# Keeping the first experts' last chunk back and adding it inside the second attention

## The chip, the cores and the metric

The kernel runs on one core of one Trainium2 chip. The metric is the device time of one execution in microseconds (us); the time given for a kernel is the median of several runs. A profiled execution of the same program gives the trace from which the lines below are copied.

## The reference

The input x has 16 batches of 256 rows of 128 channels, all in float32. Four residual steps follow each other, and each works on a layer norm of x:

```python
x = x + attn_a(layernorm(x))
x = x + ffn(layernorm(x))
x = x + attn_b(layernorm(x))
x = x + ffn(layernorm(x))
```

`attn_a` and `attn_b` are softmax attentions with 16 heads of 8 channels; `attn_b` adds a relative position term to the scores. The feed-forward step (the "experts") is the same function both times:

```python
logits = einsum('bld,ed->ble', x, gate_weight)          # 8 experts
kth    = sort(logits.reshape(-1))[4 * 128 * 6 - 1]
gates  = logits * (logits >= kth)
h      = gelu(einsum('bld,ehd->bleh', x, w1) + b1)       # 512 hidden
y      = einsum('bleh,edh->blde', h, w2) + b2
out    = einsum('blde,ble->bld', y, gates)
```

## The kernel before

**State.** x stays in SBUF for the whole kernel as 16 tiles `x0` to `x15`, one for each batch, rows on partitions. The experts work in the transposed layout, channels on partitions, in 8 chunks of two batches (512 rows): chunk 7 holds batches 14 and 15.

**Stages.** The program runs attention a, the first experts, attention b and the second experts, each in pools of its own. `experts(last, ...)` is called with `last=False` for the first and `True` for the second. For each of 64 pairs of chunk and expert (c, e) there are four hidden units (`h_unit`, line 1078: a matmul of 512 columns and a gelu on ACT, line 1080) and one output (`y_unit`, line 1089: four matmuls accumulated in a PSUM bank `py`). `gated` (lines 1201 to 1205) then adds the bias, multiplies by a broadcast row of gates `gb`, and sums into `acc` of the chunk, on DVE. The `gb` tiles come by DMA from DRAM on SP's queue (`broadcast_gates`, line 1182, seven buffers). The first 16 pairs are computed ahead, in the tail of the attention in front, and kept as `raw` tiles.

**The end of a chunk.** `residual` (lines 1225 to 1234) transposes the sum back with four transposes on PE (line 1228) into a PSUM bank `f_pr`, and adds it to the two x tiles on DVE (line 1231). For chunks 0 to 6 this is put one step later, behind the next pair's matmuls. The last pair of chunk 7 goes through `last_in_halves` (lines 1207 to 1223): its `y_unit` is done in two halves of 256 columns, and each half has its own gating (line 1217), sum (line 1220), two transposes and one add.

**Attention b.** `attention_b` opens the pool `b_w` before the first experts begin. `begin` puts the first pieces of batches 0 to 2 between the matmuls of the last 12 pairs of the first experts. `run` opens the pools `b_4` (SBUF) and `b_ps` (PSUM) after the experts' pools are closed; the first instruction that uses a bank of `b_ps` waits for the last reader of the closed PSUM pool. The order on the five engines in `run` is the order in which the code is written. It has 128 units, 8 for each batch: in a unit U, `scores` issues 16 matmuls in the 64x64 tiling of PE (line 876) into a two-bank tile `b_s` (three buffers), a maximum on DVE (line 886), and four exponentials on ACT (line 891); `turn`, written two units later, transposes the result on DVE (line 901). The dictionary `table` puts the other steps of a batch at fixed units: `first` at unit 0 of a batch (queries and keys of the next batch, line 718, into a one-bank tile `b_m`, two buffers), `second` at unit 4, and so on. x14 and x15 are read by attention b only for the layer norms and sums of batches 14 and 15.

Of the kernel before, what the change touches and what calls it, by code (L numbers as in the profile page):

```python
# [10 lines left out]
F32 = mybir.dt.float32  # L11
I32 = mybir.dt.int32
AF = mybir.ActivationFunctionType
ALU = mybir.AluOpType
# [4 lines left out]
P = 128  # L19
NB, T, C = 16, 256, 128  # L20
# [8 lines left out]
CH = 512  # L29
NCHUNK = NB * T // CH  # L30
# [48 lines left out]
def hybrid_kernel(ctx: ExitStack, tc: tile.TileContext, io):  # L79
    nc = tc.nc  # L80
# [5 lines left out]
    def load(name, shape, queue, src=None):  # L86
        t = cpool.tile(shape, F32, tag=name, name=name)
        queue.dma_start(t, io[name] if src is None else src)
        return t
# [4 lines left out]
    xs = [load("x0", [P, T // P, C], nc.sync, xr[0])]  # L94
# [23 lines left out]
    def const(name):  # L118
        lo, hi = CONSTS[name]
        return head[:, lo:hi]  # L120
# [7 lines left out]
    ident = const("ident")  # L128
# [516 lines left out]
    def attention_b(outer):  # L645
# [10 lines left out]
        wpool = outer.enter_context(tc.tile_pool(name="b_w", bufs=1))  # L656
# [24 lines left out]
        def values_tile(pool, i):  # L681

            va = pool.tile([P, NK, NJ, DH, NG], F32, tag=f"va{i}", name=f"b_va{i}")
            nc.gpsimd.memset(va, 0.0)
            vas.append(va)

        values_tile(wpool, 0)
        mask_h, mask_q = const("mask_h"), const("mask_q")
        NH2, NN = NH // 2, NQB // 2
        rows_of, xnTs, batch, vz, tall = {}, {}, {}, {}, {}  # L690
# [156 lines left out]
        def run(place, filling):  # L847
            with ExitStack() as st:
                main(st, place, filling)

        def main(st, place, filling):
            pool = st.enter_context(tc.tile_pool(name="b_4", bufs=1))
            psum = st.enter_context(tc.tile_pool(name="b_ps", bufs=1, space=PSUM))
# [44 lines left out]
            def turn(U):  # L898

                half, i = divmod(U, NU // 2)  # L900
                nc.vector.transpose(  # L901
                    pT[:, half % 2, 4 * i : 4 * i + 4].rearrange("p n k h q -> p (n k h q)"),
                    probs.pop(U).rearrange("p u r k -> p (u r k)"),
                )
# [99 lines left out]
            total = NB * NU  # L1004
# [23 lines left out]
            def for_batch(f, b, *rest):  # L1028
                if 0 <= b < NB:
                    f(b, *rest)  # L1030
# [11 lines left out]
                6: lambda b: for_batch(ahead_rows, b + 3),  # L1042
                7: lambda b: for_batch(ahead_spread, b + 1),
            }

            own_at = {0: 2, 1: 2, 2: 1, 4: 2, 5: 2, 6: 2, 8: 2, 9: 2, 10: 1, 12: 2, 13: 2}
            done = 0
            for U in range(total + 2 * NU + 1):
                b, i = divmod(U, NU)
                table.get(i, lambda b: None)(b)  # L1050
                if U < total:
                    scores(U)
                while done < min(total, U - 1):
                    turn(done)
                    done += 1
                if U >= total:
                    place["h"] = (epool, 5, psum, "ss", 3)
                    place["y"] = (psum, "ss", 3)
                    place["raw"] = (epool, 4)
                    for _ in range(own_at.get(U - total, 0)):  # L1060
                        own.append(next(filling))

        return begin, run


    def bank(psum, tag, name, bufs):
# [7 lines left out]
    def h_unit(place, c, e, k):  # L1074
        pool, bufs, psum, tag, mb = place["h"]
        ph = bank(psum, tag, f"ph{c}_{e}_{k}", mb)
        m = e * NHC + k
        nc.tensor.matmul(ph, w1[:, m * P : (m + 1) * P], xn2[c], start=True, stop=True)  # L1078
        hT = pool.tile([P, CH], F32, tag="hT", name=f"hT{c}_{e}_{k}", bufs=bufs)
        nc.scalar.activation(  # L1080
            hT, ph, AF.Gelu_apprx_tanh, bias=b1[:, m : m + 1], scale=1.0
        )
        return hT

    def y_unit(place, c, e, hs, width=CH, part=""):
        psum, tag, mb = place["y"]
        py = bank(psum, tag, f"py{c}_{e}{part}", mb)
        for k in range(NHC):
            nc.tensor.matmul(  # L1089
                py[:, 0:width], w2[:, e * NHC + k, :], hs[k], start=k == 0, stop=k == NHC - 1  # L1090
            )
        return py
# [19 lines left out]
                    yield  # L1112
            prev = (c, e, hs)

    def experts(last, place, raw, filling, middle):
        with ExitStack() as st:
            hpool = st.enter_context(tc.tile_pool(name="f_h", bufs=1))
            pool = st.enter_context(tc.tile_pool(name="f_2", bufs=2))
            psum = st.enter_context(tc.tile_pool(name="f_ps", bufs=1, space=PSUM))
# [58 lines left out]
                kth.append(f)  # L1178

            def broadcast_gates(c, e):  # L1180
                gb = pool.tile([P, CH], F32, tag="gb", name=f"gb{c}_{e}", bufs=7)
                nc.sync.dma_start(
                    gb.rearrange("p (t k) -> p t k", k=P),
                    gd[c * 4 * NE : (c + 1) * 4 * NE, :]
                    .rearrange("(t e) k -> e t k", e=NE)[e]
                    .partition_broadcast(P),
                )
                return gb

            accs = {}  # L1190

            def gated(c, e, y, bias):

                gb = broadcast_gates(c, e)
                if e == 0:
                    accs[c] = pool.tile([P, CH], F32, tag="acc", name=f"acc{c}", bufs=2)
                    dst = accs[c]
                else:
                    dst = pool.tile([P, CH], F32, tag="gy", name=f"gy{c}_{e}")
                if bias is None:  # L1200
                    nc.vector.tensor_tensor(dst, y, gb, ALU.mult)
                else:
                    nc.vector.scalar_tensor_tensor(dst, y, bias, gb, ALU.add, ALU.mult)  # L1203
                if e:
                    nc.vector.tensor_tensor(accs[c], accs[c], dst, ALU.add)

            def last_in_halves(c, e, hs):

                gb = broadcast_gates(c, e)
                pys = [  # L1210
                    y_unit(place, c, e, [h[:, half * T : (half + 1) * T] for h in hs], T, half)
                    for half in range(2)
                ]
                for half, py in enumerate(pys):
                    cols = slice(half * T, (half + 1) * T)
                    gy = pool.tile([P, CH], F32, tag="gy", name=f"gy{c}_{e}_{half}")
                    nc.vector.scalar_tensor_tensor(  # L1217
                        gy[:, cols], py[:, 0:T], b2[:, e : e + 1], gb[:, cols], ALU.add, ALU.mult
                    )
                    nc.vector.tensor_tensor(  # L1220
                        accs[c][:, cols], accs[c][:, cols], gy[:, cols], ALU.add
                    )
                    residual(c, (half,))
# [34 lines left out]
            total = NCHUNK * NE  # L1258
            prev, due, ready = None, 0, []
            for i in range(EARLY, total + 1):  # L1260
                c, e = divmod(i, NE)
                hs, now, ready = None, ready, []
                if i < total:
                    hs = [h_unit(place, c, e, k) for k in range(NHC)]
                if middle is not None and i >= total - 12 and i % 2 == 0:
                    next(middle(psum), None)
                if due < EARLY:
                    gated(*divmod(due, NE), raw[due], None)
                    due += 1
                    if due % NE == 0:  # L1270
                        ready.append(due // NE - 1)
                if i == total:
                    last_in_halves(*prev)
                elif prev is not None:
                    gated(
                        prev[0], prev[1], y_unit(place, *prev),
                        b2[:, prev[1] : prev[1] + 1],
                    )
                    if prev[1] == NE - 1:
                        ready.append(prev[0])  # L1280
                for done in now:
                    residual(done)
                prev = (c, e, hs)
            for done in ready:
                residual(done)

    epool = ctx.enter_context(tc.tile_pool(name="epool", bufs=1))
# [1 line left out]
    def fill():  # L1289

        place, raw = {}, []
        return place, raw, early(place, raw)

    ahead = fill()
    attention_a(*ahead[::2])
    with ExitStack() as st:
        begin, run = attention_b(st)
        experts(False, *ahead, begin)
        ahead = fill()
        run(*ahead[::2])  # L1300
    experts(True, *ahead, None)


def _spread(v, extra):
# [73 lines left out]
```

## Time and profile before

| what | value |
|---|---|
| time, median of 3 runs | 1542.66 us (1542.0 to 1543.3) |
| time of the profiled execution | 1539.13 us |
| its span, first to last instruction | 1537.3 us |
| granted TensorE clock, mean | 0.999 |
| first experts: last transposes (line 1228) of chunk 7 | 741.04 and 742.53 us |
| attention b: first scores (line 876) | 744.59 us |
| attention b: last turn (line 901) starts | 1082.8 us |
| busy share of the span: PE, DVE, ACT, POOL | 99%, 52%, 55%, 26% |

PE is shown as busy nearly everywhere, because the durations of pipelined matmuls are drawn long and overlap each other. The start times of instructions say more: the distance from one start to the next is what an instruction took of PE. In rows of the trace, a float32 matmul counts twice (two passes) and a transpose once, so that a `py` of four matmuls is a row of 8, and the scores of one unit are 32. In brackets behind a row stands how long the engine had been idle before it, and what ended the wait.

### The profile page before, as it was taken

To read this page: it belongs to the slowest core of one execution; us is meant where nothing else is said; L and a number is where in the kernel's file an instruction comes from. 1 tells how busy PE (TensorE), PEld (TensorE's weight loads), DVE (VectorE), ACT (ScalarE), POOL (GpSimd) and SP (SyncE) were. 2 spreads that over 40 slices of the span, in tenths; PEclk is the share of its full clock that TensorE was granted. 3 is DMA by queue.
4 is the path that set the end of the run, shared out by engine and by line. 5 is a ranking of instruction groups with operands and counts; after the bars stand their busy time and mean duration, and the time that the engine had idled before them with its cause. 6 is when DMAs were issued, how large, how long until landed. Compare 5 with 4: busy or idle time off the path is not lost. (4 is left out here: it accounts for less than half of the span.)

```text
span 1537.3 us, 30882 instructions
## 1 busy us (share of the span) xinstructions
PE 1524.0 (99%) x12292; PEld 858.5 (56%) x12292; DVE 800.1 (52%) x1624; ACT 838.7 (55%) x2092; POOL 405.9 (26%) x521
## 2 busy tenths in 40 slices
PE   9999999999999999999999999999999999999998
PEld 6777777544444444444677777777444444444444
DVE  6887877345133312121699999999353143212222
ACT  4666666644443334343688888888544433434342
POOL 6332331200001000003388988886100000000000
PEclk9999999999999999999999999999999999999999
DMA  3511110000322111111122222221002133211110
GB/s 97 156 33 29 36 36 16 2 7 4 76 71 80 50 39 38 38 41 28 24 56 58 50 51 48 55 57 37 8 1 62 44 84 82 51 45 39 44 41 7
DMA packets 174127, 69.91 MB, mean 45 GB/s; under 512 B 74520, under 2 KB 173600, under 8 KB 173728
## 3 DMA queue, kind: packets, MB, share of 16 engines
q1 hardware_dynamic: 173408, 67.54, 18.8%
q8 instruction: 97, 1.59, 0.4%
q10 hardware_dynamic: 576, 0.41, 0.1%
q14 instruction: 46, 0.38, 0.1%
HBM read 50.88 MB, written 12.58 MB: 41 GB/s over the span
## 5 line engine op out<-in xcount | busy, mean ns | idle before, releaser
L1080 ACT ACTIVATE hT<-ph,head 128x512 f32<-128x512 f32 x512 | 351.0, 687 | 419.4 <-PE ph L1078 416.9
L1078 PE MATMUL ph<-xn,w 128*128 128x512 f32 x1024 | 464.3, 594 | 1.1 <-ACT hT L1080 1.1
L1089 PE MATMUL py<-hT,w 128*128 128x512 f32 (+1 forms) x1040 | 461.1, 586 | 1.0 <-ACT logits L977 0.5
L1089 PEld LDWEIGHTS py<-hT,w 128*128 128x128 f32 x1040 | 196.6, 190 | 237.3 <-issue 230.6
L1078 PEld LDWEIGHTS ph<-xn,w 128*128 128x128 f32 x1024 | 191.4, 190 | 228.5 <-issue 224.7
L1203 DVE SCALAR_TENSOR_TENSOR gy<-py,head,gb 128x512 f32<-128x512 f32 x82 | 61.6, 751 | 425.5 <-PE py L1089 425.5
L891 ACT ACTIVATE b_pr<-b_s,b_nm 128x256 f32<-128x256 f32 x512 | 235.5, 473 | 58.7 <-DVE b_nm L886 58.4
L447 DVE TENSOR_REDUCE a_nm<-a_s 128x2 f32<-128x512 f32 x256 | 158.6, 683 | 51.8 <-PE a_t L470 50.1
L886 DVE TENSOR_REDUCE b_nm<-b_s 128x4 f32<-128x1024 f32 x128 | 152.7, 1193 | 20.9 <-PE b_s L876 20.6
L876 PE MATMUL b_s<-b_kT,b_qd 64*64 64x256 f32 x1024 | 159.8, 382 | 0.0
L901 DVE STREAM_TRANSPOSE b_pT<-b_pr 128x1024 f32<-128x1024 f32 x128 | 157.1, 1228 | 0.0
L876 PE MATMUL b_s<-strip,b_qb 64*64 64x256 f32 x2048 | 156.6, 376 | 0.0
L876 PE MATMUL b_s<-b_kS,b_qd 64*64 64x256 f32 x1024 | 156.5, 382 | 0.0
L476 ACT ACTIVATE a_pT<-a_t 128x512 f32<-128x512 f32 x256 | 132.5, 603 | 31.8 <-PE a_t L470 31.7
L470 PE MATMUL a_t<-a_qa,a_qk 32*128 32x256 f32 x1024 | 134.5, 394 | 0.7 <-DVE a_nm L447 0.6
L766 POOL TENSOR_TENSOR b_qd<-b_qsel,head 128x512 f32<-128x512 f32 x64 | 84.1, 1337 | 178.5 <-DMA b_qsel<-b_qT 169.7
L442 PE MATMUL a_s<-a_qk 32*128 32x256 f32 x1024 | 130.3, 390 | 0.4 <-DVE a_nm L447 0.4
L153 POOL TENSOR_SCALAR ve<-mv 128x2 f32<-128x2 f32 x64 | 14.8, 231 | 425.1 <-DVE mv L150 415.1
L442 PEld LDWEIGHTS a_s<-a_qk 32*128 32x128 f32 x1024 | 92.1, 185 | 23.5 <-issue 15.3
L891 ACT ACTIVATION_READ_ACCUMULATOR b_pr<-b_s,b_nm 128x1 f32 x512 | 104.3, 204 | 0.0
L470 PEld LDWEIGHTS a_t<-a_qa,a_qk 32*128 32x128 f32 x1024 | 100.1, 185 | 4.8 <-issue 1.7
L162 POOL TENSOR_SCALAR xn<-x,mv,rstd 128x128 f32<-128x128 f32 x126 | 99.7, 800 | 6.6
(175 smaller groups left out, 1430.9 us busy)
## 6 DMA issues: line engine op xcount, KB each, us to landing
gb<-gd SPq DMA_DIRECT2D x128, 256.0 KB
w<-in_w SPq DMA_DIRECT2D x2, 2048.0 KB
a_qks<-a_qkc SPq DMA_DIRECT2D x15, 256.0 KB
a_qk<-a_qks SPq DMA_DIRECT2D x60, 64.0 KB
x<-in_x SPq DMA_DIRECT2D x16, 128.0 KB
b_qs<-b_qT SPq DMA_DIRECT2D x64, 32.0 KB
b_qsel<-b_qT SPq DMA_DIRECT2D x64, 32.0 KB
b_z<-b_qs SPq DMA_DIRECT2D x16, 128.0 KB
```

The lines of the kernel that those rows point to most:

```text
L162: (last or nc.gpsimd).tensor_scalar(xn[:, t, :], xs[b][:, t, :], mv[:, t, 0:1], rstd[:, t : t + 1], ALU.subtract, ALU.mult,)
L442: nc.tensor.matmul(sc[:, t, :], q[b][rows, g, t * P : (t + 1) * P], k[b][rows, g, :], start=True, stop=True,)
L447: nc.vector.tensor_reduce(nms[G % 4][:, :, j, 0:1].rearrange("p t o -> p (t o)"), sc, AX.X, ALU.max, negate=True,)
L470: nc.tensor.matmul(sc[:, t, :], k[b][rows, g, t * P : (t + 1) * P], qaug[G][rows, :], start=True, stop=True,)
L476: nc.scalar.activation(pT, sc, AF.Exp)
L876: nc.tensor.matmul(sc[64 * c : 64 * c + 64, r, u, :], (qb_[rows, at, c] if rel else qd[rows, at, x]).rearrange("p h q -> p (h q)"), strip[ ...
L886: nc.vector.tensor_reduce(nm, sc, AX.X, ALU.max, negate=True)
L891: nc.scalar.activation(pr[:, u, r, :], sc[:, r, u, :], AF.Exp, bias=nm[:, r, u : u + 1], scale=1.0, accum_out=sums[b][:, n : n + 1],)
L901: nc.vector.transpose(pT[:, half % 2, 4 * i : 4 * i + 4].rearrange("p n k h q -> p (n k h q)"), probs.pop(U).rearrange("p u r k -> p (u r ...
L1078: nc.tensor.matmul(ph, w1[:, m * P : (m + 1) * P], xn2[c], start=True, stop=True)
L1080: nc.scalar.activation(hT, ph, AF.Gelu_apprx_tanh, bias=b1[:, m : m + 1], scale=1.0)
L1089: nc.tensor.matmul(py[:, 0:width], w2[:, e * NHC + k, :], hs[k], start=k == 0, stop=k == NHC - 1)
```

## The change

The tile `late` (512 float32 on each partition) is added to `b_w`, the pool of attention b that is open during the first experts. In the first experts, the sum of chunk 7 is built in `late` in place of a tile `acc7`. The last pair goes through `gated` with a whole `y_unit`, no longer in halves, and the first experts end there: the residual of chunk 7 is not made by them. In `run`, at U = 2 (the third unit), ahead of that unit's scores, `add_late` transposes `late` with four transposes into a `b_m` tile and adds the two halves to x14 and x15. To make room, the first experts have six `gb` buffers in place of seven. The second experts are as they were.

```diff
@@ -685,6 +685,8 @@
             vas.append(va)
 
         values_tile(wpool, 0)
+
+        late = wpool.tile([P, CH], F32, tag="late", name="b_late_sum")
         mask_h, mask_q = const("mask_h"), const("mask_q")
         NH2, NN = NH // 2, NQB // 2
         rows_of, xnTs, batch, vz, tall = {}, {}, {}, {}, {}
@@ -1042,12 +1044,28 @@
                 6: lambda b: for_batch(ahead_rows, b + 3),
                 7: lambda b: for_batch(ahead_spread, b + 1),
             }
+            def add_late():
+
+                pr = psum.tile([P, 2 * T], F32, tag="m", name="b_late", bufs=2)
+                for t in range(4):
+                    nc.tensor.transpose(
+                        pr[:, t * P : (t + 1) * P], late[:, t * P : (t + 1) * P], ident
+                    )
+                for j in range(2):
+                    b = NB - 2 + j
+                    nc.vector.tensor_tensor(
+                        xs[b], xs[b],
+                        pr[:, j * T : (j + 1) * T].rearrange("p (t c) -> p t c", c=C), ALU.add,
+                    )
+
 
             own_at = {0: 2, 1: 2, 2: 1, 4: 2, 5: 2, 6: 2, 8: 2, 9: 2, 10: 1, 12: 2, 13: 2}
             done = 0
             for U in range(total + 2 * NU + 1):
                 b, i = divmod(U, NU)
                 table.get(i, lambda b: None)(b)
+                if U == 2:
+                    add_late()
                 if U < total:
                     scores(U)
                 while done < min(total, U - 1):
@@ -1060,7 +1078,7 @@
                     for _ in range(own_at.get(U - total, 0)):
                         own.append(next(filling))
 
-        return begin, run
+        return begin, run, late
 
 
     def bank(psum, tag, name, bufs):
@@ -1112,7 +1130,8 @@
                     yield
             prev = (c, e, hs)
 
-    def experts(last, place, raw, filling, middle):
+    def experts(last, place, raw, filling, middle, late):
+
         with ExitStack() as st:
             hpool = st.enter_context(tc.tile_pool(name="f_h", bufs=1))
             pool = st.enter_context(tc.tile_pool(name="f_2", bufs=2))
@@ -1178,7 +1197,7 @@
                 kth.append(f)
 
             def broadcast_gates(c, e):
-                gb = pool.tile([P, CH], F32, tag="gb", name=f"gb{c}_{e}", bufs=7)
+                gb = pool.tile([P, CH], F32, tag="gb", name=f"gb{c}_{e}", bufs=7 if last else 6)
                 nc.sync.dma_start(
                     gb.rearrange("p (t k) -> p t k", k=P),
                     gd[c * 4 * NE : (c + 1) * 4 * NE, :]
@@ -1193,7 +1212,10 @@
 
                 gb = broadcast_gates(c, e)
                 if e == 0:
-                    accs[c] = pool.tile([P, CH], F32, tag="acc", name=f"acc{c}", bufs=2)
+                    if c == NCHUNK - 1 and not last:
+                        accs[c] = late
+                    else:
+                        accs[c] = pool.tile([P, CH], F32, tag="acc", name=f"acc{c}", bufs=2)
                     dst = accs[c]
                 else:
                     dst = pool.tile([P, CH], F32, tag="gy", name=f"gy{c}_{e}")
@@ -1269,7 +1291,7 @@
                     due += 1
                     if due % NE == 0:
                         ready.append(due // NE - 1)
-                if i == total:
+                if i == total and last:
                     last_in_halves(*prev)
                 elif prev is not None:
                     gated(
@@ -1281,7 +1303,7 @@
                 for done in now:
                     residual(done)
                 prev = (c, e, hs)
-            for done in ready:
+            for done in ready if last else ():
                 residual(done)
 
     epool = ctx.enter_context(tc.tile_pool(name="epool", bufs=1))
@@ -1294,11 +1316,11 @@
     ahead = fill()
     attention_a(*ahead[::2])
     with ExitStack() as st:
-        begin, run = attention_b(st)
-        experts(False, *ahead, begin)
+        begin, run, late = attention_b(st)
+        experts(False, *ahead, begin, late)
         ahead = fill()
         run(*ahead[::2])
-    experts(True, *ahead, None)
+    experts(True, *ahead, None, None)
 
 
 def _spread(v, extra):
```

In the built programs the order of the instructions changes in these places and no other. On PE, the eight matmuls of the two half `y_unit`s become four of 512 columns, the four transposes leave the end of the first experts, and four stand between the scores of units 1 and 2. On DVE, the last pair has one gating and one sum, and the two adds to x14 and x15 stand between the maxima of units 1 and 2. On SP's queue, the last three `gb` transfers of the first experts stand later: `gb7_5` and `gb7_6` behind the transfers `b_qs0`, `b_qsel0`, `b_z0` and `b_kS0` of attention b's batch 0, and `gb7_7` behind `b_vs0` and `b_vz0`. ACT and POOL keep their order. The two banks of `b_m` change places from the second `b_m` tile on.

## The prediction

> **What bounds the kernel now.** I read the page first, then the order of time at the seam between the first experts and attention b on PE and DVE, then the waits inside attention b.
>
> From the page, busy time by engine and the chain that ended last:
>
> ```profile
> PE 1524.0 (99%) x12292; PEld 858.5 (56%) x12292; DVE 800.1 (52%) x1624; ACT 838.7 (55%) x2092; POOL 405.9 (26%) x521
> ...
> PE 27%; DVE 1%; issue 0%; DVEq 0%
> ```
>
> The chain covers only the second experts (27% and 1% of the span), so it says nothing of the seam, and PE's 99% is drawn from overlapping durations. The seam has to be read row by row. PE in order of time:
>
> ```profile
> 735.44 5.76 PE L1089 MATMUL py<-hT,w 128*128 128x512 f32 x21
> 741.04 0.38 PE L1228 MATMUL f_pr<-head,acc 128*128 128x128 f32 x2
> 742.53 0.41 PE L1228 MATMUL f_pr<-head,acc 128*128 128x128 f32 x2 [1.11 <-DVE acc L1220]
> 743.52 1.13 PE L718 MATMUL b_m<-b_xnT,b_w 128*128 128x256 f32 x4 [0.58 <-DVE x L1231]
> 744.59 0.43 PE L876 MATMUL b_s<-b_kT,b_qd 64*64 64x256 f32 x1
> ```
>
> PE ends the last outputs at 741.20, then stands idle twice, 1.11 and 0.58 us, for the sums and adds of DVE. The first matmul of attention b (line 718) starts at 743.52, 2.32 us after the outputs. DVE at the same place, and its first maximum:
>
> ```profile
> 737.79 0.75 DVE L1203 SCALAR_TENSOR_TENSOR gy<-py,head,gb 128x512 f32<-128x512 f32 x1 [5.39 <-PE py L1089]
> ...
> 741.24 0.48 DVE L1217 SCALAR_TENSOR_TENSOR gy<-py,head,gb 128x256 f32<-128x256 f32 x1 [0.78 <-PE py L1089]
> ...
> 743.05 0.42 DVE L1231 TENSOR_TENSOR x<-x,f_pr 128x256 f32<-128x256 f32 x1 [0.66 <-PE f_pr L1228]
> 746.67 1.22 DVE L886 TENSOR_REDUCE b_nm<-b_s 128x4 f32<-128x1024 f32 x1 [3.20 <-PE b_s L876]
> ```
>
> Line 718 starts 0.05 us after the last add ends (743.05 + 0.42 = 743.47): the add to x15 is the last reader of the closed PSUM pool. Inside attention b the waits from 765 to 1090 us show who paces it:
>
> ```profile
> ACT b_pr L891 <- DVE b_nm L886: 55.9, 117, 1.4
> DVE b_nm L886 <- PE b_s L876: 16.5, 27, 0.9
> ```
>
> ACT waits 117 times for DVE's maximum; DVE itself waits only 16.5 us of 325. In the windows view DVE is busy 93.83 of the 100 us from 900 to 1000. Attention b is paced by DVE, and the seam by the turns between PE and DVE.
>
> **The change, part by part.**
>
> *The seam.* What is removed is the way from the last output through sum, transposes and add, at the end of the first experts. A whole `py` takes as long as two halves: eight passes started at 734.15 and the next eight at 737.58, 3.43 us later, and the two halves ended at 741.20. The whole `py7_7` therefore starts at 737.58. Pair 6 of the chunk began its gating 3.64 us after its outputs began (734.15 to 737.79), so the new gating starts at 741.22 and ends 0.75 later, at 741.97. It is now the last reader of the PSUM pool, and in the built program line 718 waits for it and for nothing of the sum. With the same 0.05 us behind it, line 718 starts at 742.02 in place of 743.52: **1.50 us earlier**. The sum that follows (0.69 us) ends by 742.7, ahead of the first maximum at 746.67 - 1.50 = 745.17; the idle 3.20 us in front of that maximum hide it. If PE did not have to wait at all, the most to be had is 2.32 us.
>
> *The four transposes on PE, now between the scores of units 1 and 2.* Inside the experts, four transposes take 0.44 us from start to start (695.28 to 695.72 before the next hidden unit). Here they stand between matmuls of the 64x64 tiling. The nearest rows are the visit between units 3 and 4:
>
> ```profile
> 751.26 0.61 PE L876 MATMUL b_s<-strip,b_qb 64*64 64x256 f32 x8
> 751.80 0.71 PE L786 MATMUL b_m<-b_w,b_xnT 128*128 128x128 f32 x4
> 752.35 0.38 PE L707 MATMUL b_m<-head,xn 128*128 128x128 f32 x2
> 752.66 0.43 PE L876 MATMUL b_s<-b_kT,b_qd 64*64 64x256 f32 x1
> ...
> 752.94 0.38 PE L876 MATMUL b_s<-b_kS,b_qd 64*64 64x256 f32 x2
> ```
>
> The last group of scores takes 0.54 us up to the visit, against 0.43 from unit 1 into unit 2 (747.66 to 748.09): 0.11 for the way in. Two transposes (one row each, 0.11 us by the 0.44 for four) need 0.22 of the 0.31 us from 752.35 to 752.66: 0.09 for the way out. The first group behind takes 0.28 against 0.22: 0.06 more. So 0.44 + 0.11 + 0.09 + 0.06 = **0.70 us**. Bounds: 0.44 if the changes of tiling cost nothing, 1.03 for the whole longer visit above (0.55 + 0.31 + 0.11 + 0.06). I take 0.70, which has the same shape on both sides. They wait for nothing: `late` is finished at 742.7, and unit 1 ends at 748.09 - 1.50 = 746.59.
>
> The Trainium skill, page "TensorEngine Tiling (Array Packing)", section "Key Properties", speaks against this place: changing the tiling mode drains TensorE. By that rule the price is above the plain 0.44, and the 0.26 us around the visit agree. The skill's page "TensorE: Matmul & The Clock Gate", Part 4, gives about 275 ns for a 128x128 transpose inside a kernel; an estimate by that figure is 4 x 0.275 = 1.10 us, and the sum below would be near zero. The trace draws 273 ns for one as well, but starts the next after 0.11, and the starts decide here.
>
> *The two adds on DVE, now between the maxima of units 1 and 2.* A pair takes 0.74 us (the row at 696.15). Before, DVE had an idle 0.50 us there, since the maximum at 750.06 waited for the scores of unit 2; these come 0.70 later relative to unit 1, so 1.20 us are free for 0.74. Cost nothing; cover left 0.46. If the transposes cost only 0.44 the cover still holds (0.94); with no cover at all the pair would cost 0.74, since behind it DVE's order is full. Queued behind the adds are the maximum of unit 2, the first turn, and through them ACT's exponentials.
>
> *Waits that come with it.* The second half of unit 4's visit (line 707) now uses the bank of `b_late` and waits for the add to x15: that add ends near 748.8, the matmuls come at 752.35 - 0.80. No cost. POOL's memset of `b_va1` (743.14, 0.95 us) waits for the sum in place of the transposes, ends earlier, and nobody needs it for batch 0.
>
> *Six gate buffers, and SP's queue.* In the 13 units in which a `raw` and a `py` are gated together, a buffer comes back after three units of 6.87 us less one gating of 0.75: 19.9 us; the closest case, near 468, is some 16 us. The slowest landing seen is 5.7 us (first issue at 384.35, first gating at 390.07, seven transfers at once). Later there are six units, 41 us. `gb7_5` goes out at 693.1 behind `b_kS0`, `gb7_6` waits for the gating at 695.48 as `gb7_7` did, and `gb7_7` goes out at 704.2, when the gating at 703.45 has ended; it is needed at 741.2. What it has passed, `b_vs0` and `b_vz0`, goes out as before; behind it only the transfers of batch 1 wait, until after 743. Cost nothing; cover 14 us.
>
> **Sum.** -1.50 + 0.70 + 0 = **-0.80 us**. From unit 2 on, everything hangs on DVE's maximum of that unit (750.06, now 749.26), on the turns behind it and on PE's order, all earlier by 0.80, and the order of later instructions is unchanged, so the shift goes to the end. The profiled execution has 1539.13 us with a span of 1537.3; the sum makes 1538.3 and 1536.5. The median of the runs is 1542.66, 3.5 us above the profiled execution, so I carry only the difference over: 1542.66 - 0.80 = 1541.9. With the bounds of the transposes the change is -1.06 to -0.47.
>
> **Rivals.**
>
> *More is gained (chance 0.12).* The matmuls of line 718 follow the outputs without the gating's wait (2.32), or the transposes vanish beside waits (1.50): -1.5 to -2.3 us, 1540.4 to 1541.2. For it: attention b is paced by DVE, so time on PE may be free. Against: at unit 2 DVE waited for PE in the trace (0.50 us).
>
> *The transposes cost more than the seam gives (0.10).* Place: between units 1 and 2. The drawn durations are paid one after another, 4 x 0.273 = 1.09, with the idle of the weight loads around the visit (0.39 ahead of line 786, 0.17 ahead of line 876): 1.65 us. It decides from 1.50 on. Then +0.15, and with DVE's pair uncovered (0.74) +0.9: 1542.8 to 1543.6, slower than before. Against: start distances in every such row are shorter than durations.
>
> *Attention b changes its step (0.12 faster, 0.10 slower).* Its 128 maxima and turns take 1.185 and 1.227 us, 309 us in all, and the new tile moves the SBUF tiles behind it by 2048 bytes; its waits of DVE on PE are 16.5 us over some 14 batches. One per cent of the first, or a fifth of the second, is 3.1 us: 1539.6 or below, or, in the other direction, 1545.8 or above. For it: DMA landings, POOL (87.69 busy of 100 us) and DVE interlock. Against: the turns keep within 1.190 and 1.236 us over buffers at different addresses, and with fixed orders and durations a delay of 0.70 can push nothing later by more than that and the pair's 0.74. A gate ring that starves belongs here too: it needs landings above 16 us plus DVE's idle 4.3 us per unit, against 5.7 seen.
>
> **How the numbers follow.** About 0.2% (3.1 us) is what a measurement of this kernel can tell from no change. The forecast has 0.56; with the first two rivals 0.78 lie within 0.2%, 0.12 are faster and 0.10 slower. The range runs from the best of the first rival, 1540.3, to the worst of the second, 1543.6, widened by the spread of the runs around their median (0.65 each way): 1539.6 to 1544.3. The forecast alone, with the same spread, is 1540.9 to 1542.8.
>
> **What the profile after would show.** Right: line 718 near 742.0, one idle of about 0.8 us on PE in place of two; about 0.7 us more between the scores of units 1 and 2; the two adds ahead of a maximum that still waits for PE; the last turn near 1082.0; the experts up to 737.6 unchanged. Wrong: a wait for `gb` in the first experts, a maximum of unit 2 that starts with the end of the adds, or a last turn that has moved by another amount than line 718 and the transposes together make.

## The result, and the profile after

The changed kernel's median is 1538.53 us (19 executions, 1536.52 to 1541.37) against 1542.48 us for the kernel before beside it (19 executions): a ratio of 0.9981 with a 95% interval of 0.9974 to 0.9988. The forecast was 1541.9. Over all executions of this study the means are 1541.21 us for before (131) and 1538.95 us for the changed kernel (30): 2.25 us less, plus or minus 0.50 (95%, as everywhere below). The runs were made in several sets, on at least three chips. Only the kernel before was measured beside every set, so a difference between kernels of different sets can hold a difference of chips as well. The profiled execution of the changed kernel has 1539.97 us and a span of 1538.2.

The page after shows as little of the seam as the one before:

```profile
PE 1526.8 (99%) x12284; PEld 859.6 (56%) x12284; DVE 799.3 (52%) x1622; ACT 839.0 (55%) x2092; POOL 405.9 (26%) x521
...
PE 27%; DVE 1%; issue 0%; DVEq 0%
```

PE at the seam in order of time (start, duration, engine, line, operation, tile; in brackets the idle time before it and what ended it). The lines of attention b have moved: queries 718 to 720, scores 876 to 878, maximum 886 to 888.

```profile
735.98 7.03 PE L1107 MATMUL py<-hT,w 128*128 128x512 f32 x16
743.85 1.13 PE L720 MATMUL b_m<-b_xnT,b_w 128*128 128x256 f32 x4 [0.84 <-DVE gy L1225]
744.91 0.43 PE L878 MATMUL b_s<-b_kT,b_qd 64*64 64x256 f32 x1
...
747.99 0.61 PE L878 MATMUL b_s<-strip,b_qb 64*64 64x256 f32 x8
748.53 0.65 PE L1051 MATMUL b_late<-head,b_late_sum 128*128 128x128 f32 x4
749.11 0.43 PE L878 MATMUL b_s<-b_kT,b_qd 64*64 64x256 f32 x1
```

One idle time of 0.84 us is left of the 1.11 and 0.58. The four transposes stand between units 1 and 2 and hold the scores back by 0.58 us. DVE at the same place:

```profile
739.62 0.75 DVE L1225 SCALAR_TENSOR_TENSOR gy<-py,head,gb 128x512 f32<-128x512 f32 x1 [5.39 <-PE py L1107]
...
743.05 0.75 DVE L1225 SCALAR_TENSOR_TENSOR gy<-py,head,gb 128x512 f32<-128x512 f32 x1 [1.96 <-PE py L1107]
...
747.01 1.22 DVE L888 TENSOR_REDUCE b_nm<-b_s 128x4 f32<-128x1024 f32 x1 [2.49 <-PE b_s L878]
...
749.81 0.74 DVE L1056 TENSOR_TENSOR x<-x,b_late 128x256 f32<-128x256 f32 x2
751.14 1.23 DVE L888 TENSOR_REDUCE b_nm<-b_s 128x4 f32<-128x1024 f32 x1 [0.59 <-PE b_s L878]
```

The two adds are over before the scores of unit 2, whose maximum still waits 0.59 us for PE. The whole execution is 1.83 us late here: pair 6's gating starts at 739.62, before at 737.79. That delay is older than the seam, and the windows view of the first 32 us says where it comes from (columns: stretch, its length, busy time of PE, PEld, DVE, ACT and POOL, granted clock, DMA share, GB/s; the first row is before, the other two are the changed kernel):

```profile
24.00:28.00 4.00, 4.00 (x26) 2.92 (x22) 3.88 (x10) 2.17 (x4) 2.63 (x5) 0.60 0.02 2
```

```profile
20.00:24.00 4.00, 4.00 (x19) 2.54 (x14) 0.70 (x2) 0.65 (x2) 2.23 (x4) 0.50 0.36 63
24.00:28.00 4.00, 3.88 (x29) 3.44 (x28) 3.89 (x10) 1.19 (x2) 1.00 (x3) 0.50 0.04 7
```

TensorE's clock was granted at one half for 3.41 us in the one execution (24.8 to 28.2) and for 10.24 us in the other (19.7 to 29.9). The code there is the same in both. Measured from pair 6's gating, line 720 comes 1.50 us earlier than line 718 did, unit 2's maximum 0.75 us, and the end of the span 0.97 us. Unit 2's maximum before the change, for this comparison:

```profile
750.06 1.23 DVE L886 TENSOR_REDUCE b_nm<-b_s 128x4 f32<-128x1024 f32 x1 [0.50 <-PE b_s L876]
```

The waits inside attention b, 766 to 1091 us, are as before:

```profile
ACT b_pr L893 <- DVE b_nm L888: 55.8, 117, 1.4
...
DVE b_nm L888 <- PE b_s L878: 16.4, 27, 0.8
```

So this trace bears out a gain of 0.97 us, and the measurement says 2.25. The experiments look for the rest.

### The profile page after: what moved, and what is told of

It is laid out like the page before. It is cut to its first block, busy times and chain, and to the rows that moved or that the text cites. A ratio compares the mean times of both kernels' runs of the same rounds, so it can differ in the third digit from the quotient of the medians.

```text
span 1538.2 us, 30864 instructions
## 1 busy us (share of the span) xinstructions
PE 1526.8 (99%) x12284; PEld 859.6 (56%) x12284; DVE 799.3 (52%) x1622; ACT 839.0 (55%) x2092; POOL 405.9 (26%) x521
```

## Experiments

**Both kernels again, and both with an even clock at the start.** Theory A: the seam is worth about 1 us and the rest is the clock of the first 30 us. Theory B: all of it is the change. The second pair has 14 dummy matmuls (matmuls whose result nobody reads) at the start, so that the clock does not fall there:

```diff
-                        together(maxima(0, bank8("a_mx0")[:, 0]))
+                        mx = bank8("a_mx0")
+                        stoke(mx, 2)
+                        together(maxima(0, mx[:, 0]))
...
-                together(maxima(1, bank8("a_mx1")[:, 0]))
+                mx = bank8("a_mx1")
+                stoke(mx, 4)
+                together(maxima(1, mx[:, 0]))
...
+                if G in (2, 3):
+                    stoke(sc, 1)
...
+            def stoke(t, count):
+
+                for _ in range(count):
+                    nc.tensor.matmul(
+                        t[:, 0], wS["w"][:, 0:P], wS["w"][:, 0:T], start=True, stop=True
+                    )
```

> The kernel before, unchanged, run beside itself: it shows how far two sets of runs of one program lie apart, and it gives the granted clock of each run. Theory A (the seam is worth about 1.0 us, and the rest of the 3 to 4 us between the medians is the TensorE clock granted in the first 30 us, which differs from run to run): ratio near 1, runs spread over some 4 us, span falls by about 1.0 us for each 0.001 of mean clock. Theory B (the whole 3 to 4 us are the change itself): no such line; runs spread over less than 1.5 us at one clock and the same at another.

> The changed kernel again, with the granted clock of each run. Theory A: at equal mean clock its span is 1.0 us (0.7 to 1.3) below that of the kernel before; the medians may differ by anything from 0 to 4 us, as the clocks fall. Theory B: 3 to 4 us below at equal clock.

> The kernel before with 14 more dummy matmuls of 256 columns, between 15 and 25 us of the span, where PE otherwise waits for DVE, so that the granted clock does not fall there. Theory A: the half-clock windows near 20 to 30 us go or become fewer, mean clock 0.999 to 1.000 in nearly all runs, spread under 1.5 us, median 1 to 3 us below the kernel before unless the dummies themselves cost as much (up to 1.5 us). Theory B says nothing of it: the same spread and median as before, plus what the dummies cost.

> The changed kernel with the same 14 dummy matmuls. Theory A: 1.0 us (0.7 to 1.3) below the kernel before with the dummies, with a narrow spread. Theory B: 3 to 4 us below it.

Measured: before again 1541.18 us (12 executions), the changed kernel again 1538.61 (11), ratio to before 0.9983 (0.9975 to 0.9992). With the dummies before has 1545.32 (8) and the changed kernel 1543.07 (11); their start is at full clock, in before's trace it takes about 4.7 us more, and the mean spans are 1543.22 and 1541.34. So 1.9 us (plus or minus 0.7) remain with an even start, where theory A allowed 1.3 at most. A fit of span on mean clock over the 74 spans of the plain kernels gives 1.65 us (plus or minus 0.24) at equal clock: theory A is too small, and theory B's 3 to 4 us is too much. The trace of before again showed what neither had. PE at its seam, and the windows view of 746 to 750:

```profile
743.88 0.41 PE L1228 MATMUL f_pr<-head,acc 128*128 128x128 f32 x2 [1.11 <-DVE acc L1220]
744.87 1.63 PE L718 MATMUL b_m<-b_xnT,b_w 128*128 128x256 f32 x4 [0.58 <-DVE x L1231]
746.43 0.69 PE L876 MATMUL b_s<-b_kT,b_qd 64*64 64x256 f32 x1
```

```profile
746.00:750.00 4.00, 4.00 (x47) 2.21 (x48) 0.34 (x1) 2.22 (x3) 0.00 (x0) 0.65 0.16 17
```

The program and the idle times are the same as in the first trace of before, but line 718 takes 1.63 us in place of 1.13 and the first scores 0.69 in place of 0.43: the clock was at one half from 745.37 to 748.78. From pair 6's gating to the first turn, this seam took 1.64 us longer than in the first trace. The clock records of the trace change only in steps of whole windows of 3.413 us (13.65, 10.24, 716.8 and 3.41 us in this execution). The Trainium skill, page "TensorE: Matmul & The Clock Gate", Part 1, tells of such a free-running window of about 3.4 us and of two clock levels, and the trace agrees. By the same Part 1 of the Trainium skill the clock falls after a whole idle window, by which the 1.69 us of idle here would have cost nothing; the measurement decides. That made a new theory, the window theory: the two idle times of before together bring a half-clock window if one window happens to cover them.

**The seam's idle time filled, and opened.** In the first kernel three dummies fill the longer of PE's two idle times in before (the 0.58 us stays); in the second, copies on VectorE make it longer in the changed kernel.

```diff
                 pr = psum.tile([P, 4, C], F32, tag="m", name=f"f_pr{c}_{halves[0]}", bufs=2)
+                if c == NCHUNK - 1 and not last:
+                    for _ in range(2 - halves[0]):
+                        nc.tensor.matmul(
+                            pr[:, 2 * halves[0] : 2 * halves[0] + 2, :], ident,
+                            xn2[0][:, 0:T], start=True, stop=True,
+                        )
```

> The kernel before, with TensorE's two idle times at the seam filled by dummy matmuls (256 columns each: two ahead of the transposes of the first half of chunk 7, one ahead of those of the second half, into the bank that the transposes then overwrite). Window theory: TensorE's clock is granted in windows of 3.41 us, and one in which TensorE idles about 1.7 us is followed by one at half clock. The kernel before idles 1.11 + 0.58 us between 741.42 and 743.52, so that a window covers both in (3.41 - 2.10) / 3.41 = 0.38 of its executions, and each of those pays the 1.64 us that the repeated kernel before showed there. Filled, nothing on the path moves, no execution pays: mean span 1539.24 (44 executions of before so far) - 0.38 x 1.64 = 1538.6, executions with a mean clock of 0.996 or less fall from 19 in 44 to about 1 in 6 (after: 5 in 30), ratio about 0.9996. Rival (the clock at the seam has no part): 1539.2, ratio 1.0000, clocks as before.

Measured: 1539.72 us (12 executions), ratio to before 0.9991 (0.9982 to 0.9999). In the trace line 718 stands where it stood against pair 6's gating, and the clock there is 1.00. The rival's 1.0000 is just outside the interval, and the mean is 1.14 us (plus or minus 0.95) below that of before beside it on the same chip: dummy work that does nothing made the kernel faster, by an amount that is poorly known. One part of the expectation did not show. Of the kernel's 12 executions 3 had a mean clock of 0.996 or less, and of before's 29 beside it 7, the same share.

```diff
+                if c == NCHUNK - 1 and e == NE - 1 and not last:
+                    for j in range(2):
+                        idle = pool.tile([P, CH], F32, tag="gb", name=f"idle{j}", bufs=6)
+                        nc.vector.tensor_copy(idle, y)
                 if e:
                     nc.vector.tensor_tensor(accs[c], accs[c], dst, ALU.add)
```

> The changed kernel, with two copies of the last expert output (128x512) on VectorE between its gating and its addition, so that line 720's matmuls wait longer: idle of 0.84 + 2 x about 0.75 (a 128x512 gating's time) = 2.3 us. Window theory: a window holds 1.6 us of that in (3.41 + 2.3 - 3.2) / 3.41 = 0.74 of executions, which then pay about 1.6 us at half clock: mean span 1537.17 (30 executions of after so far) + 1.5 + 0.74 x 1.6 = 1539.9, a mean clock of 0.996 or less in over half of the executions, and most likely half clock at 746 to 749 in the trace. Rival (the clock at the seam has no part): + 1.5 alone, 1538.7, and clocks as after's (0.996 or less in 5 of 30).

Measured: 1540.96 us (11 executions), mean span 1538.85. The idle time became 2.13 us, and the path to the end of the trace 1.35 us longer, with no half clock behind it:

```profile
743.22 1.10 PE L720 MATMUL b_m<-b_xnT,b_w 128*128 128x256 f32 x4 [2.13 <-DVE idle L1229]
744.25 0.43 PE L878 MATMUL b_s<-b_kT,b_qd 64*64 64x256 f32 x1
```

The mean is 1.68 above the changed kernel's, not 2.7. A mean clock of 0.996 or less, expected in over half of the executions, came in 2 of 11. This one went the rival's way, though its mean says little: the changed kernel was not measured beside it. The kernel with the transposes moved ahead (below) was; this mean is 2.43 us (plus or minus 1.1) above that one's, and the traces account for 1.56 of it. By itself the experiment left the window theory open: the clock at the start varies too much to read the seam's windows from an execution's mean clock. The next two steps therefore use the kernels with the dummies at the start.

**The same, with an even start.** First the kernel before with both sets of dummies, then the changed kernel with five and with three copies, then before again for its share. The only new edits are the counts of copies:

```diff
-                    for j in range(2):
+                    for j in range(5):
```

```diff
-                    for j in range(2):
+                    for j in range(3):
```

> The kernel before with the dummies at the start that keep the clock at 1.0 there, and the dummies at the seam. With those at the start alone 3 of 8 executions had a mean clock of 0.999 (one window at half clock somewhere) and 5 had 1.000; after with them 1 of 11. Window theory: that window is the seam's, and filled it is gone: 0.999 in at most 1 of 11 executions, mean span 1543.22 - 3/8 x 1.64 = 1542.6 or a little less. Rival (the window lies elsewhere): 3 to 5 of 11 at 0.999, mean span 1543.2.

> The changed kernel with the dummies at the start, and five copies of the last expert output on VectorE, so that TensorE idles 0.84 + 5 x 0.645 = 4.06 us at the seam (two copies gave 2.13). Window theory: half clock follows a window of 3.41 us with less than about 1.1 to 1.3 us of matmuls other than transposes (the repeated before: 1.09 and half clock; before: 1.42, after with two copies: 1.72, neither). With 4.06 us of idle that holds in (4.06 + 2 x 1.1 - 3.41) / 3.41 = 0.84 or more of executions: mean clock 0.999 in most of them, and 0.5 in the trace's windows behind 742. Spans 1541.34 + 3.2 = 1544.6 without and 1546.2 with it. Rival (idle of this length has no part in the clock): 1.000 throughout, 1544.6.

> The same with three copies: 0.84 + 3 x 0.645 = 2.77 us of idle. Window theory: a share of (3.41 - 2.77 + 2 x 0.46) / 3.41 = 0.46 (0.57 with the limit at 1.3 us) has the window: 0.999 in about half of the executions, spans 1543.3 without and 1544.9 with it. Rival: 1.000 throughout, 1543.3.

> The kernel before with the dummies at the start, repeated for the share of its executions with a window at half clock: 3 of 8 so far, against 1 of 11 for after and 1 of 11 (and one of 0.997) for before with the seam filled. Window theory: a window holds under 1.1 to 1.3 us of matmuls beside transposes in 0.37 to 0.48 of executions: 3 to 5 of 11 at 0.999, these 1.6 us longer than the rest, mean span about 1543.2. Rival: at most 1 of 11, and a mean span of 1542.5 or less.

| kernel with the dummies at the start | idle at the seam, us | executions | at clock 1.000 | mean span, us |
|---|---|---|---|---|
| before (both runs) | 1.11 + 0.58 | 18 | 9 | 1543.28 |
| before, seam filled | 0.58 | 11 | 9 | 1542.58 |
| changed | 0.84 | 11 | 10 | 1541.34 |
| changed, three copies | 2.73 | 6 | 2 | 1544.93 |
| changed, five copies | 3.92 | 5 | 0 | 1545.90 |

With five copies no execution keeps the full clock, and the trace shows the window right behind the idle time (PE, then the windows view):

```profile
749.66 1.11 PE L733 MATMUL b_m<-b_xnT,b_w 128*128 128x256 f32 x4 [3.92 <-DVE idle L1242]
750.70 0.69 PE L891 MATMUL b_s<-b_kT,b_qd 64*64 64x256 f32 x1
```

```profile
750.00:754.00 4.00, 4.00 (x36) 2.37 (x38) 0.12 (x1) 2.22 (x3) 0.95 (x1) 0.58 0.16 16
```

Against pair 6's gating, the idle time alone taken off, unit 2's maximum is 1.60 us late in this trace and 1.65 in that with three copies, which has such a window too. With three copies the two executions at 1.000 have 1542.9 and 1543.1 us, the three at 0.999 have 1545.03 in the mean, and one at 0.996 has 1548.5, unexplained. So idle time at the seam brings the window, and how often grows with its length. Both rivals' "1.000 throughout" are out.

Not every 0.999 is the seam's: the trace from the second set of before with the dummies has its half clock at the very end (1539.8 on, 4.5 us), with a span of 1542.1. Of before's nine executions below 1.000, two have such short spans (1542.1 and 1542.4), and seven have 1543.7 to 1545.2 (1544.34 in the mean), against a mean of 1542.68 for the nine at 1.000. Counted by length, about 7 in 18 had a window inside, which fits the expected 0.37 to 0.48; the mean span came as forecast (1543.2), and with the seam filled too (1542.6). This share is an estimate. Neither trace of before with the dummies has the window at the seam, and the difference to the filled seam, 0.70 us (plus or minus 0.75, on another chip), does not exclude zero.

The half-clock records of a trace fix its grid of windows. The idle time, as drawn, inside the window ahead of the scores was then 1.70 us (before again, the trace with the window at 745.37), 1.97 (three copies) and 2.45 (five copies), each followed by half clock, and 1.49 (before) and 1.68 (two copies), each not. Three more traces of before's seam or a variant with the same waits held at most 1.04, 1.28 and 1.42 us in one window and had no half clock there: with the two traces of before above that makes one in five. If the limit is near 1.7 us, only a window that covers both idle times of before, from 741.42 to 743.52, reaches it, and (3.41 - 2.10) / 3.41 = 0.38 of all positions do. The kernel with two copies would reach it in (3.41 + 2.13 - 3.38) / 3.41 = 0.63.

But drawn idle time alone does not fix a limit. At the end of the second trace of the changed kernel a window (1530.50 to 1533.91) held 1.76 us, and the clock stayed at full through the next (columns as above):

```profile
1530.50:1533.90 3.40, 1.65 (x9) 1.05 (x7) 1.85 (x5) 0.00 (x0) 0.00 (x0) 1.00 0.14 39
1533.90:1536.40 2.50, 0.00 (x0) 0.00 (x0) 0.00 (x0) 0.00 (x0) 0.00 (x0) 1.00 0.18 52
```

And in the first 30 us half clock followed windows with as little as 0.3 us of idle. What the clock counts as work stays open.

**The transposes: left out, and moved ahead of unit 0.** The first kernel leaves out the transposes and adds of the last chunk; the second moves them behind line 720.

```diff
-                if U == 2:
-                    add_late()
```

```diff
-                if U == 2:
+                if U == 0:
                     add_late()
```

> The changed kernel without the four transposes and two additions of the last chunk (two batches keep their values without the experts' share). Forecast's sum: unit 2's maximum 0.70 earlier against the end of the gating, and the rest of the kernel with it. By the trace of after the first two transposes start 0.11 and 0.58 apart and the scores behind them 0.28 later, about 0.75. Rival: VectorE, not TensorE, sets unit 2, and less than 0.3 is gained.

> The changed kernel, with the four transposes and two additions placed ahead of unit 0's scores, right behind line 720's 128x128 matmuls, instead of between units 1 and 2. Forecast's sum: the same four transposes cost 0.44, the tiling switch of 0.26 to 0.3 is gone, and the additions fill VectorE's 2.49 us wait for the first scores: first scores 0.44 later, unit 2's maximum 0.3 earlier, mean span 1537.17 - 0.3 = 1536.9. Rival: the first scores are what everything waits for, so that 0.44 stays on the path and what is saved later is nothing: mean span 1537.2 to 1537.6.

> The changed kernel with the transposes ahead of unit 0's scores and the dummies at the start, for its price at an even clock: the traces gave 0.20 less than the changed kernel, so 1541.36 - 0.2 = 1541.15 at clock 1.000. Rival (nothing gained): 1541.35.

Measured: without them (one execution, by its trace) the first turn comes 0.74 us earlier than in the changed kernel, against pair 6's gating, and the end 0.66. That is their whole price. Ahead of unit 0 they cost less. PE and DVE of that kernel:

```profile
740.39 1.13 PE L720 MATMUL b_m<-b_xnT,b_w 128*128 128x256 f32 x4 [0.84 <-DVE gy L1225]
741.36 0.60 PE L1051 MATMUL b_late<-head,b_late_sum 128*128 128x128 f32 x4
741.89 0.43 PE L878 MATMUL b_s<-b_kT,b_qd 64*64 64x256 f32 x1
```

```profile
742.07 0.75 DVE L1056 TENSOR_TENSOR x<-x,b_late 128x256 f32<-128x256 f32 x2 [1.00 <-PE b_late L1051]
743.92 1.23 DVE L888 TENSOR_REDUCE b_nm<-b_s 128x4 f32<-128x1024 f32 x1 [1.10 <-PE b_s L878]
```

The scores start 1.50 us after line 720 in place of 1.06, so 0.44 is paid, as inside the experts, where no tiling changes either; the adds lie in the wait for the first scores. The first turn is 0.31 us earlier, the end 0.21. The median is 1538.28 (12 executions), ratio to before 0.9985 (0.9977 to 0.9994); with the dummies at the start the mean at clock 1.000 is 1541.16 against 1541.36. This is the best version tried, by 0.2 us in the trace and in the mean at clock 1.000, which is less than a comparison of medians can tell.

**Two orders that failed.** In some traces a POOL result came late inside attention b. In the first trace of before with dummies, POOL and then PE:

```profile
1065.36 2.12 POOL L819 COPY b_va<-b_vz 32x256 f32<-32x256 f32 x3 [1.67 <-DMA b_vz<-b_vs]
...
1073.53 1.58 POOL L162 TENSOR_SCALAR xn<-x,mv,rstd 128x128 f32<-128x128 f32 x2
```

```profile
1075.16 0.33 PE L720 MATMUL b_m<-head,xn 128*128 128x128 f32 x1 [0.45 <-POOL xn L162]
```

A late DMA holds POOL's copy, POOL's masks and rows follow late, PE waits for the rows in the fifth unit, and the maximum behind it is 0.92 us later than in before's trace. Two kernels put these rows ahead of the masks, the second with the transposes at unit 0; a third, built on the second, also put unit 0's scores ahead of the queries.

```diff
-                if b:
-                    for_batch(ahead_masks, b, 1)
                 visit(
...
                 for_batch(gate_rows, b - 2)
+                if b:
+                    for_batch(ahead_masks, b, 1)
```

```diff
+                if U == 0:
+                    scores(0)
                 table.get(i, lambda b: None)(b)
                 if U == 0:
                     add_late()
-                if U < total:
+                if 0 < U < total:
                     scores(U)
```

> The kernel before, with one order changed on GpSimd in attention b: in each batch's first visit the normalised rows for the gate (1.58 us of xn and 0.95 us ahead of it) go before the batch's second masks (4.9 us) instead of behind them. In the trace of before these rows are done 0.35 us before TensorE transposes them in the fifth unit; in one execution of before with a stoked start they came 1.0 us too late (a copy of the values waited 1.67 us for its DMA), and everything behind was 0.92 us later. Stall theory: such stalls cost an execution of before about 0.5 us in the mean and after less; with the rows 5 us earlier no stall is left, and mean span falls from 1539.13 (73 executions of before) to about 1538.6, most of it in the spread. Rival (the stalls are too rare to count): 1539.1.

> The changed kernel with its transposes ahead of unit 0's scores (as in the run before: mean span 1536.42) and the gate's rows ahead of the second masks on GpSimd. Stall theory: little is left to gain in this kernel, 0 to 0.3 us; mean span 1536.1 to 1536.4. Rival: masks that end 2.5 us later make unit 4's scores wait in each of 15 batches, and it is slower by over 1 us.

> As g2, with unit 0's scores ahead of line 720's queries and the four transposes. TensorE has 0.84 us of idle to lose (line 720 waits for the last gating to read its bank) and gains one more change of tiling, 0.26 to 0.3: unit 2's maximum about 0.5 earlier, span 0.5 less than g2. Rival: the scores' banks are those that the gating still reads, the wait stays and the tiling change is paid: 0.3 more than g2.

Measured: mean spans 1548.46, 1546.44 and 1547.93. The first is 9.6 us longer than before beside it, and the other two 10.0 and 11.5 us longer than the kernel with the transposes at unit 0 (1536.42, on another chip). The masks were the tighter of the two, as the second kernel's waits from 766 to 1091 us say. Without the new order the maxima waited 16.0 us for PE, and the weight loads not at all for POOL:

```profile
DVE b_nm L888 <- PE b_s L878: 27.3, 27, 2.4
...
PEld b_s L878 <- POOL b_qb L776: 11.1, 20, 0.9
```

So the share of such stalls could not be measured this way. In the third kernel the wait at the seam stays (0.94 us ahead of the scores, for the last reader of their bank) and its first turn is 0.37 us later than the second's: no gain there either.

## Why the prediction was wrong, point by point

- **The seam, -1.50: right.** Line 720 came 1.50 us earlier against pair 6's gating, with one idle time of 0.84 us (forecast about 0.8), on the gating and not on the sum.
- **The transposes, +0.70: right, 0.05 low.** The way in took 0.11 (747.99 to 748.53 against 0.43), the transposes and the way out 0.58, the slower first group behind them 0.06: 0.75 at unit 2. The plain 0.44 is what they cost where no tiling changes, and the rest is put down to the change of tiling. The rule of the Trainium skill's page "TensorEngine Tiling (Array Packing)", "Key Properties", and the row agreed. The estimate of 1.10 us from the 275 ns of the Trainium skill's page "TensorE: Matmul & The Clock Gate", Part 4, was too high: the four and the way out took 0.58 us together.
- **The adds, buffers, SP's queue, waits: right.** The maximum of unit 2 waits 0.59 us for PE after the adds; the experts' gating waits for `py` and not for `gb`.
- **The sum, -0.80: right in what it covers.** -0.75 at unit 2, and 0.2 us more in small steps over attention b: -0.97 at the end, inside the bounds of -1.06 to -0.47. That these steps made it -0.97 was not foreseen. With the seam filled in before and an even start, the two kernels differ by 0.94 at clock 1.000 (1542.30 and 1541.36, on two chips).
- **What failed is the last step: "so I carry only the difference over".** It took 1542.66 as the base and the 3.5 us between the profiled execution and this median as something that the change could not touch. Both were wrong.
- **The base was high.** 1542.66 was the median of three executions, and the median of 131 is 1541.34. The 0.65 taken for the spread was those three; single executions of before lie between 1537.6 and 1543.7. With 1541.34 the same sum gives 1540.5 and the same bounds 1538.3 to 1543.0, which hold the measured 1538.53. That would have been luck: the gain is 2.25 us in the means, and the sum has 0.80.
- **A term was missing.** For the most part the 3.5 us are half-clock windows: the fit above gives 0.90 us for each 0.001 of mean clock, and executions of before lie between 0.995 and 1.000, the profiled one at 0.999. Most of these windows lie in the first 30 us, which both kernels share, but some belong to the seam. The sum put PE's idle time at nothing but its length. In one trace of before the two idle times brought a half-clock window of 1.64 us. By the count above it comes in about 7 of 18 executions, an estimated 0.64 us in the mean, and in none of the changed kernel's traces without copies. Filling the longer idle time gave 0.70 (plus or minus 0.75, on another chip) with an even start and 1.14 (plus or minus 0.95) without. The first profile could not show it: its window covered 1.49 us of idle.
- **What the miss is made of.** The forecast of 1541.9 lies 3.4 us above 1538.53. The base is 1.3 of it, the window term about 0.6 and the small steps 0.2. Of the remaining 1.2, 0.4 is that 1538.53 lies below the mean of all thirty executions (1538.95); the rest is open.
- **The rivals.** "More is gained" (-1.5 to -2.3 us) has the size of the difference in the means, but by luck, not the way: PE's wait did not vanish. None of the transposes' price was hidden, nor did it exceed 1.50. "Attention b changes its step" did not happen in the profiled execution (waits of 55.8 and 16.4 against 55.9 and 16.5).
- **What stays open.** -0.97 and the estimated -0.64 make -1.61. The comparisons give -1.94 (plus or minus 0.54) with an even start and -2.25 (plus or minus 0.50) without, so 0.3 to 0.6 us have no proven cause; the first could be chance, the second is just outside its interval. A candidate is the stalls behind late DMAs. From the first turn to the last, against the best trace of their kind, six traces of before and its variants lost 0, 0, 0.36, 0.65, 0.81 and 1.36 us inside attention b. Of nine traces of the changed kernel and its variants seven lost 0.1 or less, one 0.48 and one 0.6. Only one of these stalls was followed to its DMA, no reason is known why the changed kernel should have fewer, and the experiments on them failed.

## What to carry to other kernels

Take the base of a forecast from many executions: the median of three was 1.3 us off here, more than the change that was forecast. Idle time of TensorE can have a second price: with 1.7 to 2.5 us of it in one 3.4 us window the next window ran at half clock in three traces, in some executions of a program and not in others. So look at the granted clock of several executions before carrying a difference from one trace to a median. And a step of 128x128 transposes goes next to other 128x128 work: there it cost 0.44 us, between 64x64 matmuls 0.75.

## What the runs showed of the hardware

- At the seam, windows of 3.413 us with 1.70, 1.97 and 2.45 us of drawn idle time on TensorE were followed by half clock, and windows with 1.49 and 1.68 us were not; at the end of a kernel one with 1.76 us was not either. Behind the seam such a window cost 1.60 to 1.65 us (three traces).
- In the first 30 us the clock was at one half for one to three windows in the traces of the two kernels (one and three in the two of before), although PE is drawn busy for 3.2 us or more of each 4 us from 12 us on. What sets it there was not tried.
- Dummy matmuls can pay: three of them in waiting time took 1.14 us (plus or minus 0.95) off the mean of the kernel before. 14 at the start made the kernel before 4.7 us later at the seam.
- POOL's order in attention b had no room here: with the gate's rows ahead of the second masks the kernels were about 10 us longer.
